# A two-layer graph network on one core: the adjacency's transpose goes from TensorE to VectorE, by way of a second load and DRAM

## The chip, the cores and the metric

The kernel runs on one core of a Trainium2 chip. The metric is the device time of one execution in microseconds (us): before the change a median of 2358.65 us over 3 runs, 2358.03 to 2359.63. A profile is one execution recorded by the hardware profiler. A core has five engines that work through their own instruction lists in order and wait for each other by semaphores: TensorE (PE in the profile, PEld its weight loads), VectorE (DVE), ScalarE (ACT), GpSimd (POOL) and SyncE (SP), which here only issues transfers. TensorE writes its results to PSUM banks, the other data lie in SBUF (128 partitions), and 16 DMA engines move data between SBUF and DRAM.

## The reference

Two layers over B = 16 graphs of N = 1024 nodes with C = 256 channels, all float32. Both share one adjacency `adj` (1024 x 1024).

```python
# layer 0
h = relu(layernorm(x))                       # (16, 1024, 256)
c = mean(h, channel)                         # one number per node
A = (1 - |2 sigmoid(c_j - c_i) - 1|)         # by pairs of nodes, symmetric
g = relu((h^T @ (adj * A)) * para)           # queries
k, v = split(h @ kv_w)                       # keys, values
x = x + softmax(g_head @ k_head^T * scale) @ v_head     # 4 heads
# layer 1
h = relu(layernorm(x))
An = adj + I
deg = colsum(An) + rowsum(An) - diag(An)
agg = (An * deg^-1/2[:, None] * deg^-1/2[None, :]) @ h
x = x + batchnorm(relu(batchnorm(agg @ W1^T + b1)) @ W2^T + b2)
```

Layer 0 uses the rows of `adj` as they lie. Layer 1 needs the transposed, scaled adjacency as the moving operand of TensorE (the tile `ahatT`), and W1 and W2 transposed.

## The kernel before

The batches are taken one after the other. For each there is a graph stage (weights times the rows of h: `f_gps`), keys and values (`f_kps`, `f_vps`), attention in four steps (a half of the queries times a pair of heads: scores `f_s`, exponentials `f_p`, values `f_o`), and a first linear layer of layer 1 for the batch (`linear1`). The second half of the network follows when all batches are through. The order of the instructions on every engine is the order in which the program emits them: the stages run under a manual schedule, and what an engine is to do between the parts of a stage is handed in as lists of steps.

In batch 0 the head runs thus:

- SP loads x of batch 0 in four parts, the eight row blocks of `adj` (`adj_t`, 128 rows each, which stay in SBUF for all batches), kv_w, x of batch 1 and W1 by rows (`load_rows`).
- `graph(0, between)` goes over eight blocks c of nodes. Block c needs a weight tile `w_0_c`: ScalarE makes two activations (L353, L356), VectorE multiplies by the rows of adj (L370), and TensorE makes four products of 128 x 512 (L492). The list `between[c]` holds the steps emitted ahead of block c: weights of later blocks, `turn_h(0)` (h transposed for keys and values, 32 transfers half on SP and half on POOL), and the turns of the adjacency.
- A turn of adjacency block i (`turn_adj` L1372, or `turn_adj_aside` L1383 in other banks) is eight TensorE transposes of 128 x 128 into PSUM. `place_adj` (L1380) or `place_adj_aside` (L1394) copies the result into `ahatT`, in an order of nodes in which node 8u + i lies at place 128 i + u. Seven of the eight copies are VectorE's, one is ScalarE's.
- W1 is turned by VectorE in blocks of 32 x 32 (`turn_weights`, L1452), stored to DRAM by POOL in an order that completes the transpose (L1458), and loaded back by SP into `w1T` (L1491).
- Row sums of the adjacency (L1402, ScalarE, eight) run in `between[4]`.
- After the eight blocks, `graph` runs keys and values of batch 0 (L516 to L552): 14 products in two groups V and K, with ScalarE copies and VectorE additions that free the few PSUM banks.
- `prepare_row(1)` (L307) sends the sums of h of batch 1 to DRAM and loads them back as a row over all partitions, both on SP (L315, L316). The weights of batch 1 use this row in attention step 0 of batch 0.
- Then SP loads x of batch 0 again (`again(0)`, emitted in `between[6]`) and W2 by rows (`w2n`). POOL runs `diagonal()` (L1411: sixteen small operations that pick the diagonal out of `ahatT` and add the identity), VectorE sums it, and POOL loads six small columns (`later`).

In attention of batch 0 the lists `hooks[i]` add work at the end of the scores of step i: weights of batch 1 in steps 0 and 1, two column sums of `ahatT` on ScalarE in every step (L1407), in step 1 the turn of W2 by VectorE (L1452), stored by POOL, in step 2 the sums of W1's blocks (`make_w1_sums`), in step 3 `roots`, which makes deg^-1/2. The row of roots and the scaling of `ahatT` lie in the graph stage of batch 1. VectorE's list for one step is: six additions of exponentials, the hooks, the last addition (L899), a transpose and a reduction of the sums (L907, L915), and the transpose of the step's result out of PSUM (L936), which frees the bank that the values of the next step write.

Pools of tiles hand out buffers in turn: `w4` has five (weights, para, W1, W2), `p` eight (exponentials and others), `oT` two, `att` one, and PSUM has `s` with three double banks, `t` and `o` with one bank each.

Of the kernel before, what the change touches and what calls it, by code (L numbers as in the profile page):

```python
# [10 lines left out]
F32 = mybir.dt.float32  # L11
# [6 lines left out]
P = 128  # L18
# [11 lines left out]
def fast_path(  # L30
# [38 lines left out]
    w1T_d = dram.tile([P, CC, F1], F32, tag="fw1T", name="fw1T")  # L69
    w2T_d = dram.tile([P, FC, C], F32, tag="fw2T", name="fw2T")  # L70
    w1s_d = dram.tile([P, 4, FC * P // 2], F32, tag="fw1s", name="fw1s")
# [108 lines left out]
    with ExitStack() as stage:  # L180
# [19 lines left out]

        adj_t = []
# [105 lines left out]
        def prepare_row(b, behind=lambda: None):  # L307
# [6 lines left out]
            if b > 0:  # L314
                nc.sync.dma_start(row_d[b].rearrange("(c p) -> p c", p=P), sums_of[b])  # L315
                nc.sync.dma_start(row, row_d[b].unsqueeze(0).to_broadcast([P, N]))  # L316
                return
# [155 lines left out]
        def graph(b, between):  # L473
# [42 lines left out]
            if b == 0:  # L516
# [8 lines left out]
                K.copy(0, 0)  # L525
                V.product(6)
# [9 lines left out]
                K.copy(1, 0)  # L536
                V.product(4)
# [13 lines left out]
                K.copy(0, 1)  # L551
                return qT, kT, v  # L552
# [819 lines left out]
        def turn_adj(i):  # L1372
            ps = ps_s.tile([P, NC, P], F32, tag="s", name=f"f_adjps_{i}")
            for m in range(NC):
                nc.tensor.transpose(ps[:, m, :], adj_t[i][:, ts(m, P)], ident)
            turned_adj[i] = ps

        turned_adj = {}

        def place_adj(i, copy):  # L1380
            copy(columns(i), turned_adj.pop(i).rearrange("p m (q i) -> p m i q", i=NC))

        def turn_adj_aside(i):  # L1383

            turned_adj[i] = [
                ps_o.tile([P, NC // 2, P], F32, tag="o", name=f"f_adjpsa_{i}"),
                ps_t.tile([P, NC // 2, P], F32, tag="t", name=f"f_adjpsb_{i}"),
            ]
            for m in range(NC):
                nc.tensor.transpose(  # L1390
                    turned_adj[i][m // 4][:, m % 4, :], adj_t[i][:, ts(m, P)], ident
                )

        def place_adj_aside(i, copy):  # L1394
            for n, ps in enumerate(turned_adj.pop(i)):
                copy(columns(i)[:, 4 * n : 4 * n + 4], ps.rearrange("p m (q i) -> p m i q", i=NC))
# [14 lines left out]
        def diagonal():  # L1411
# [5 lines left out]
            nc.vector.tensor_reduce(diag, on, AX.X, ALU.add)  # L1417
# [44 lines left out]
        with tc.manual_schedule(engines={ENG.PE, ENG.Activation, ENG.DVE, ENG.Pool, ENG.SP}):  # L1462
# [16 lines left out]
            turn_adj(0)  # L1479
            xs[1] = load_x(1)  # L1480
            prepare_row(0, lambda: place_adj(0, nc.vector.tensor_copy))
            turn_adj(1)
            turn_adj_aside(2)
            place_adj(1, nc.vector.tensor_copy)
            weights(0, 1)

            w1n = load_rows(W1, FC, "w1")
            w1T = big.tile([P, CC, F1], F32, tag="w1T", name="f_w1T")

            def load_w1T():  # L1490
                nc.sync.dma_start(w1T, w1T_d)  # L1491
# [5 lines left out]
                    1: [  # L1497
                        lambda: place_adj_aside(2, nc.vector.tensor_copy),
                        lambda: weights(0, 3),
                        lambda: turn_adj(3),  # L1500
                        lambda: place_adj(3, nc.scalar.copy),
                    ],
                    2: [
                        lambda: weights(0, 4),
                        lambda: turn_weights(w1n, unused("w1Q"), w1T_d, FC),
                        lambda: prepare_start(1),
                        lambda: turn_adj_aside(4),
                        lambda: place_adj_aside(4, nc.vector.tensor_copy),
                    ],
                    3: [  # L1510
                        lambda: weights(0, 5),
                        lambda: turn_adj(5),
                        lambda: place_adj(5, nc.vector.tensor_copy),
                    ],
# [1026 lines left out]
```

## Time and profile before

| what | us |
|---|---|
| median of 3 runs | 2358.65 |
| the profiled execution: its own time | 2359.59 |
| its span | 2357.7 |
| TensorE's first transpose of the adjacency | 8.26 |
| first product of the graph stage of batch 0 | 14.41 |
| first product of keys and values | 46.91 |
| first scores of attention, batch 0 | 59.26 |
| first product of the graph stage of batch 1 | 115.60 |
| first product of linear1, batch 0 | 157.82 |

The page gives the busy time of each engine as a share of the span, then the chain of work that ended last, followed back from the last instruction. The answers in order of time have one line for a run of like instructions: start, busy time, engine, line of the kernel, operation, output and inputs, shapes, count, and in brackets the idle time before it and what ended that. The answers by stretch have one line for a stretch of time: its ends, its length, the busy time of PE, PEld, DVE, ACT and POOL with the number of instructions in brackets, the granted clock of TensorE, the share of the 16 DMA engines that was busy, and the GB/s that they moved.

### The profile page before, as it was taken

What the parts mean: (1) busy time and instruction counts of PE and PEld (TensorE: products, weight loads), DVE (VectorE), ACT (ScalarE), POOL (GpSimd) and SP (SyncE); (2) the same over time, 40 slices, a digit from 0 to 9 for tenths busy, and PEclk for the clock granted to TensorE, in tenths of its full rate; (3) what the DMA queues carried; (4) which work ended last, traced back from release to release, by engine and by line L of the source; (5) the groups of instructions that cost most, each with busy time, mean ns of one, the idle gap of its engine ahead of it and who ended that gap; (6) DMA issues with size and microseconds to landing.
All of it is one profiled execution on the core that took longest, in us unless ns stands there. A gap on an engine that the chain in (4) does not pass through costs nothing.

```text
span 2357.7 us, 25774 instructions
## 1 busy us (share of the span) xinstructions
PE 2319.9 (98%) x8256; PEld 1030.6 (44%) x8256; DVE 1994.6 (85%) x2937; ACT 1416.0 (60%) x2057; POOL 447.7 (19%) x573
## 2 busy tenths in 40 slices
PE   8999999999999999999999999999999999999995
PEld 5353444434353534444443434343444434444444
DVE  7988989798979899897989798988989898747766
ACT  7846566574738474655657384746556575346644
POOL 5121222121221122221212221221212121100000
PEclk9999999999999999999999999999999999999998
DMA  7143433434342435335343324253343521455579
GB/s 205 46 143 99 150 127 124 153 110 124 136 132 73 168 90 174 103 134 143 116 143 126 116 97 154 83 177 99 134 143 116 161 72 55 135 209 174 171 242 382
DMA packets 169218, 326.42 MB, mean 138 GB/s; under 512 B 34929, under 2 KB 102001, under 8 KB 169073
## 3 DMA queue, kind: packets, MB, share of 16 engines
q1 hardware_dynamic: 145264, 268.02, 33.3%
q0 software_dynamic: 19200, 39.88, 6.4%
q10 hardware_dynamic: 4608, 16.78, 1.7%
q8 instruction: 67, 1.10, 0.2%
q14 instruction: 79, 0.64, 0.1%
HBM read 203.96 MB, written 101.77 MB: 130 GB/s over the span
## 4 chain that ended last, share of the span: by engine, by line
PE 96%; DMA 1%; DVE 1%; ACT 0%; issue 0%; SPq 0%; ACTq 0%; POOLq 0%; DVEq 0%; POOL 0%
PE f_s L871 19%; PE f_o L923 19%; PE f_aps L1088 16%; PE f_gps L689 8%; PE f_zps L1198 7%; PE f_gpsx L689 6%; PE f_zx L1760 4%; PE f_zm L1760 3%; PE f_vpsx L436 2%; PE f_kpsx L431 2%; PE f_gps L492 2%; PE f_vps L436 2%; PE f_kps L431 2%; PE f_zps L1281 1%; PE f_zps3a L1198 1%; PE f_zps3b L1198 1%
## 5 line engine op out<-in xcount | busy, mean ns | idle before, releaser
L879 ACT ACTIVATE f_p<-f_s 128x1024 f32<-128x1024 f32 x512 | 476.9, 1047 | 59.8 <-PE f_s L871 59.8
L871 PE MATMUL f_s<-f_qT,f_kT 64*128 64x512 f32 x2048 | 456.8, 596 | 0.0
L923 PE MATMUL f_o<-f_p,f_v 128*64 128x512 f32 x2048 | 453.6, 595 | 0.0
L871 PEld LDWEIGHTS f_s<-f_qT,f_kT 64*128 64x128 f32 x2048 | 191.2, 185 | 263.7 <-issue 118.1
L923 PEld LDWEIGHTS f_o<-f_p,f_v 128*64 128x64 f32 x2048 | 141.4, 137 | 304.3 <-issue 265.4
L366 POOL TENSOR_TENSOR f_w<-f_w,f_adj 128x1024 f32<-128x1024 f32 x56 | 132.3, 2363 | 700.8 <-ACT f_w L365 506.6
L991 POOL DMA_DIRECT2D f_att<-f_oT x256 | 136.1, 539 | 342.9 <-DVE f_oT L974 337.3
L894 DVE TENSOR_TENSOR f_acc<-f_acc,f_p 128x1024 f32<-128x1024 f32 x128 | 155.8, 1217 | 4.6 <-ACT f_p L879 4.6
L894 DVE TENSOR_TENSOR f_sums<-f_sums,f_p 128x1024 f32<-128x1024 f32 x128 | 155.7, 1217 | 0.0
L353 ACT ACTIVATE f_w<-f_row,f_col 128x1024 f32<-128x1024 f32 x127 | 147.3, 1160 | 12.0 <-DMA f_row<-frow 7.4
L356 ACT ACTIVATE f_w<-f_w 128x1024 f32<-128x1024 f32 x127 | 134.4, 1058 | 4.0
L1088 PE MATMUL f_aps<-f_ahatT,f_hs 128*128 128x512 f32 x256 | 115.2, 593 | 0.0
L1088 PE MATMUL f_aps<-f_ahatT,f_h_b 128*128 128x512 f32 x256 | 112.6, 592 | 0.0
L1088 PE MATMUL f_aps<-f_t,f_hs 128*128 128x512 f32 x256 | 112.5, 592 | 0.0
L365 ACT ACTIVATE f_w<-f_w,f_now 128x1024 f32<-128x1024 f32 x56 | 64.3, 1148 | 77.5 <-DVE f_now L363 77.5
L689 PE MATMUL f_gps<-f_w,f_h_a 128*128 128x512 f32 x224 | 109.8, 592 | 0.0
L885 DVE TENSOR_TENSOR f_acc<-f_p,f_p 128x1024 f32<-128x1024 f32 x64 | 77.9, 1217 | 24.9 <-ACT f_p L879 24.9
L891 DVE TENSOR_TENSOR f_sums<-f_p,f_p 128x1024 f32<-128x1024 f32 x64 | 78.1, 1221 | 20.2 <-ACT f_p L879 20.1
L370 DVE SCALAR_TENSOR_TENSOR f_w<-f_w,f_adj 128x1024 f32<-128x1024 f32 x71 | 88.0, 1258 | 7.8 <-ACT f_w L356 7.7
L285 ACT ACTIVATE f_h_a<-f_x,f_shift_a,f_rstd_a 128x256 f32<-128x256 f32 x126 | 73.8, 587 | 31.4 <-DVE f_shift_a L270 31.4
L1221 ACT ACTIVATE f_z<-f_zps,f_b 128x512 f32<-128x512 f32 x60 | 37.9, 683 | 75.3 <-PE f_zps L1198 75.3
L285 ACT ACTIVATE f_h_b<-f_x,f_shift_b,f_rstd_b 128x256 f32<-128x256 f32 x128 | 66.2, 592 | 25.8 <-DVE f_shift_b L270 25.8
(297 smaller groups left out, 3983.9 us busy)
## 6 DMA issues: line engine op xcount, KB each, us to landing
f_t<-ft SPq DMA_DIRECT2D x84, 512.0 KB, 9.6
fz<-f_z SPq DMA_DIRECT2D x64, 512.0 KB, 9.8
f_x<-in_x_dram SPq DMA_DIRECT2D x31, 1024.0 KB, 6.3
f_zb<-fz SPq DMA_DIRECT2D x42, 512.0 KB, 4.4
fx<-f_x SPq DMA_DIRECT2D x16, 1024.0 KB, 4.4
fgs<-f_gs POOLq DMA_DIRECT2D x28, 512.0 KB, 3.0
fhT<-f_hQ POOLq DMA_DIRECT2D x112, 128.0 KB, 3.2
f_hT<-fhT SPq DMA_DIRECT2D x28, 512.0 KB, 6.3
```

The costliest lines, as they stand in the source:

```text
L285: nc.scalar.activation(self.h[:, c, :], self.xt[:, c, :], AF.Relu, bias=self.shift[:, c : c + 1], scale=self.rstd[:, c : c + 1], accum_out ...
L353: nc.scalar.activation(w, rows[b], AF.Abs, bias=cols[b][:, c : c + 1], scale=0.5 / C)
L356: nc.scalar.activation(w, w, AF.Tanh)
L689: nc.tensor.matmul(ps, left, right, start=fresh and n == 0, stop=(n == PAIRS - 1), skip_group_check=more,)
L871: nc.tensor.matmul(ps[:, e, :], kT[rows_e, pair, ts(m, P)], qT[rows_e, pair, ts(g, 512)], start=True, stop=True,)
L879: nc.scalar.activation(p, ps, AF.Exp)
L894: nc.vector.tensor_add(to, to, p)
L923: nc.tensor.matmul(o_of[s][e * HD : (e + 1) * HD, :], v[:, m, ts(2 * pair + e, HD)], p[:, e, :], start=(m == 0), stop=(m == NC - 1),)
L991: queue.dma_start(t[ts(j, 32), :, a].rearrange("r h c i -> r h (c i)"), oT[ts(a, 32), :, j].rearrange("r h c i -> r h (c i)"),)
L1088: nc.tensor.matmul(ps, left[:, m, :], right(m), start=not more and m == 0, stop=(m == KH - 1), skip_group_check=more,)
L1198: nc.tensor.matmul(ps[i], left[:, ts(i, P)], right, start=not more, stop=True, skip_group_check=more,)
L1760: nc.tensor.matmul(ps, left[:, m, :], right[:, m, :], start=start and m == 0, stop=(m == 1), skip_group_check=not start,)
```

## The change

The adjacency is no longer turned by TensorE. While the graph stage of batch 0 ends and keys and values are made, SP loads the whole adjacency a second time: eight tiles, each by four transfers of 32 rows, that take every eighth row. VectorE turns each tile in blocks of 32 x 32 into `ahatT`, which serves as a staging place: two turns ahead of the products of keys and values, two in "first", one in "then", three in "end". After turns 3 and 7, POOL stores half of it to a DRAM tensor `adjT_d` in pieces of 512 bytes, four transfers a half. SP loads `adjT_d` back into `ahatT` in four transfers, and behind these x of batch 0 and W2. W1 is loaded behind the first x, turned by TensorE at the place of the first adjacency block, and copied by VectorE straight to `w1T`. The row of batch 1 goes over POOL's queue. The row sums are spread (three in block 4, one in keys and values, two each in steps 0 and 1), the column sums lie in steps 2 and 3 (four each), the six small columns come ahead of the diagonal on POOL, and the diagonal's reduction goes to step 3.

```diff
+        w1T = big.tile([P, CC, F1], F32, tag="w1T", name="f_w1T")
+        w1n = w4.tile([P, FC, C], F32, tag="w4", name="f_w1n")
+        nc.sync.dma_start(w1n, W1.rearrange("(f p) d -> p f d", p=P))
...
             if b > 0:
-                nc.sync.dma_start(row_d[b].rearrange("(c p) -> p c", p=P), sums_of[b])
-                nc.sync.dma_start(row, row_d[b].unsqueeze(0).to_broadcast([P, N]))
+                queue = nc.gpsimd if b == 1 else nc.sync
+                queue.dma_start(row_d[b].rearrange("(c p) -> p c", p=P), sums_of[b])
+                queue.dma_start(row, row_d[b].unsqueeze(0).to_broadcast([P, N]))
...
                 K.copy(0, 0)
+                for step in between["first"]:
+                    step()
...
                 K.copy(1, 0)
+                for step in between["then"]:
+                    step()
...
                 K.copy(0, 1)
+                for step in between["end"]:
+                    step()
...
-        def turn_adj(i):
...
-        def place_adj(i, copy):
...
-        def turn_adj_aside(i):
...
-        def place_adj_aside(i, copy):
...
+        stage_rows = ahatT.rearrange("p m x -> p (m x)").rearrange("p (k t r) -> p k t r", k=32, t=NC)
+        by_rows = adj.rearrange("(u i) d -> i u d", i=NC)
+        def load_adj(t, home):
+            pool, tag, bufs = home
+            to = pool.tile([P, N], F32, tag=tag, name=f"f_adjr_{t}", bufs=bufs)
+            for a in range(4):
+                nc.sync.dma_start(to[ts(a, 32)], by_rows[2 * a + t // 4, ts(t % 4, 32)])
+            adj_rows[t] = to
+        def load_adj_ahead():
+            for t, home in enumerate(((ow, "oT", 2), (ow, "oT", 2), (ow, "att", 1))):
+                load_adj(t, home)
+        def load_adj_behind():
+            for t in range(3, NC):
+                load_adj(t, (w4, "w4", 5))
+        def turn_adj(t):
+            nc.vector.transpose(
+                stage_rows[:, :, t], adj_rows.pop(t).rearrange("p (k s) -> p k s", s=32)
+            )
+        def store_adj(half):
+            to = adjT_d.rearrange("(k s) (a g x) -> g a s k x", s=32, a=4, g=2)[half]
+            for a in range(4):
+                nc.gpsimd.dma_start(
+                    to[a],
+                    stage_rows[ts(a, 32), :, 4 * half : 4 * half + 4].rearrange(
+                        "p k t r -> p k (t r)"
+                    ),
+                )
+        def reload_adj():
+            whole = adjT_d.rearrange("(m p) x -> p m x", p=P)
+            for m in range(0, NC, 2):
+                nc.sync.dma_start(ahatT[:, m : m + 2], whole[:, m : m + 2])
...
-            turn_adj(0)
+            w1ps = ps_s.tile([P, CC, FC, P], F32, tag="s", name="f_w1ps")
+            for d in range(CC):
+                for f in range(FC):
+                    nc.tensor.transpose(w1ps[:, d, f, :], w1n[:, f, ts(d, P)], ident)
...
-                    6: [
-                        lambda: prepare_end(1),
-                        make_key_sums,
-                        load_w1T,
-                        lambda: again(0),
-                    ],
-                    8: [lambda: prepare_row(1)],
+                    4: [lambda: weights(0, 7), *(lambda m=m: row_sums(m) for m in range(3))],
+                    6: [load_adj_ahead, lambda: prepare_end(1), make_key_sums],
+                    8: [
+                        load_adj_behind,
+                        lambda: turn_adj(0),
+                        lambda: turn_adj(1),
+                        lambda: prepare_row(1),
+                    ],
+                    "first": [lambda: turn_adj(2), lambda: turn_adj(3), lambda: store_adj(0)],
+                    "then": [lambda: turn_adj(4), lambda: row_sums(3)],
+                    "end": [
+                        *(lambda t=t: turn_adj(t) for t in range(5, NC)),
+                        lambda: store_adj(1),
+                    ],
                 },
             )
+            reload_adj()
+            again(0)
             w2n = load_rows(W2, CC, "w2")
             w2Q, w1s_t = (w4.tile([P, N], F32, tag="w4", name=f"f_{n}") for n in ("w2Q", "w1s"))
-            diagonal()
             for load in later:
                 load()
+            sum_diagonal = diagonal()
...
-                            hooks.setdefault(m // 2, []).append(lambda m=m: column_sums(m))
+                            hooks.setdefault(2 + m // 4, []).append(lambda m=m: column_sums(m))
+                        for m in range(4, NC):
+                            hooks[1 - m // 6].append(lambda m=m: row_sums(m))
+                        hooks[3].append(sum_diagonal)
                         hooks[1].append(lambda: turn_weights(w2n, w2Q, w2T_d, CC))
```

## The prediction

> **What bounds the kernel now.** I read the page's busy row and the end of the chain first, then the first 165 us of each engine in order of time, then the DMA rates in short stretches.
>
> ```profile
> PE 2319.9 (98%) x8256; PEld 1030.6 (44%) x8256; DVE 1994.6 (85%) x2937; ACT 1416.0 (60%) x2057; POOL 447.7 (19%) x573
> PE 96%; DMA 1%; DVE 1%; ACT 0%; issue 0%; SPq 0%; ACTq 0%; POOLq 0%; DVEq 0%; POOL 0%
> ```
>
> TensorE is the chain: only what removes TensorE work, or makes it wait, counts. In order of time, TensorE's head:
>
> ```profile
> 8.26 1.94 PE L1375 MATMUL f_adjps<-f_ident,f_adj 128*128 128x128 f32 x8 [8.26 <-DMA f_adj<-in_adj_dram]
> 12.24 1.04 PE L1375 MATMUL f_adjps<-f_ident,f_adj 128*128 128x128 f32 x8
> ...
> 14.41 3.67 PE L492 MATMUL f_gps<-f_w,f_h_a 128*128 128x512 f32 x8 [0.26 <-DVE f_w L339]
> 17.91 1.04 PE L1375 MATMUL f_adjps<-f_ident,f_adj 128*128 128x128 f32 x8
> 18.79 3.60 PE L492 MATMUL f_gps<-f_w,f_h_a 128*128 128x512 f32 x8
> ...
> 59.26 7.14 PE L871 MATMUL f_s<-f_qT,f_kT 64*128 64x512 f32 x32
> ...
> 94.50 7.09 PE L923 MATMUL f_o<-f_p,f_v 128*64 128x512 f32 x32
> ```
>
> The first three blocks of the adjacency (8.26, 12.24, 13.11) are turned while TensorE waits for the first weights anyway (0.26 on L339 remains). Blocks 3 to 7 stand between products.
>
> **What it removes.** Starts of those five are 0.88, 1.10, 0.87, 0.87 and 0.87 us ahead of the next product (17.91 to 18.79, 22.58 to 23.68, and so on): 4.6 us off TensorE. The eight W1 transposes take the place of block 0 at 8.26, before TensorE waits for the sums at 9.99: nothing. The gap at 12.24 becomes idle, since the first weights (L339, 13.58) hang on ScalarE and the row copy, not on TensorE: nothing won there. The cover holds if the weights keep up with one product per 3.5 us: ScalarE makes a block in 2.13 us (starts 14.06, 16.19, 18.32) and VectorE masks it in 1.2, with six PSUM copies of 1.2 us and W1's turn (1.24) fewer to do. W1's way through DRAM goes too (SP 5.1 us, POOL 2.5 us of issue), all of it beside TensorE: nothing. So attention starts at 59.26 - 4.6 = 54.7. That is the whole gain, 0.19% of 2358.65; 0.2% (4.7 us) is about what a measurement of this kernel can tell from no change.
>
> **The second load.** SP issues 32 transfers of 128 KB behind the two of para (31.8, 32.3). Nearest row for the issue: f_w2n, 0.42 each; for the rate, the stretch in which only w2n (32 partitions a transfer, as here) is moving:
>
> ```profile
> 12.00:14.00 2.00, 2.00 (x20) 1.91 (x18) 1.59 (x3) 1.94 (x4) 0.00 (x0) 1.00 1.04 424
> 63.00:64.00 1.00, 1.00 (x6) 0.38 (x4) 0.69 (x1) 1.00 (x2) 0.00 (x0) 1.00 1.00 242
> ```
>
> The last number is GB/s, the one before it the DMA share: the engines are full at 242 with 32 partitions, and at 424 with the 128 partitions of the first adjacency load. The Trainium skill, SBUF — State Buffer, section "Door 1: The DMA port swizzle", says that 32 partitions reach only half of the ports and gives 189 GB/s at 1 MiB, 218 at best. A tile of 0.52 MB takes 2.2 us by the row and 2.8 by the rule; I take the row, and keep the rule for the range, as it speaks against this change.
>
> From 33.1 (first bytes of para): para 2.8, then tiles at 38.2, 40.4, 42.6, the key sums' store 1.4, tiles 3 to 7 at 46 to 55, each landing 0.7 later. VectorE's deadlines: turns 0 and 1 stand ahead of the two para products (L521), which free the bank of K's first product (TensorE 44.2 after the change), so tile 1 must land by 41.7 (it does at 41.1; 0 to 0.7 us at risk). Turns 2 and 3 stand ahead of K.add(0,0,2) and the V.adds that free the bank for K.product(4) at 52.9: tile 3 by 49.7. Turn 4: by 53.3. A turn is 1.2 us (f_w2Q below, 1.24). VectorE has over 5 us of waits between 47 and 58, so these turns fit: nothing. The last three follow K's last add (54.8) and end at T7 = 58.6, delaying the first attention sums by about 1 us, which its waits of 1.73 and 0.61 there absorb.
>
> **The way back, where the cost is.** store_adj(1) goes out at T7. Each half is 2.1 MB in pieces of 512 bytes, 32 partitions a transfer: at 230 GB/s (between 200, fw2T's 256-byte pieces at full share, 131 to 184 GB/s at shares 0.7 to 0.9, and 242) 9.1 us, after 2 us of POOL's issue (fw2T: 0.74 with half the pieces, first bytes 0.5 later). SP's reload waits for all eight stores, R = 58.6 + 2 + 9.1 + 0.7 = 70.4. But the first half is stored from about 48 to 60 while tiles 4 to 7 are still loading. Sharing costs: the 1 MB load of x lands after 5.5 us at 44.0, and after 10.2 at 197.1 beside three stores of 512 KB, with 400 GB/s of both together. Loads, row and first store add up to 33 us of full DMA, 33.1 to 66.5; fully shared, tile 7 comes at 64 and R = 76.5. I take R = 74.
>
> Behind the reload in SP's order stand x of batch 0 and w2n. Bytes after R: 4.2 MB at 405 GB/s (stretches of the first load) 10.4 us, x 1.05 MB at 331 (46 to 48 us) 3.2, w2n 2.2, first bytes 1.3, landing 0.7, and 1 for the six columns of small pieces (0.5 of the DMA share after 50 us before): 18.8. So w2n lands at L = 93 (89 to 96 by the two ends of R). Before, it was there by 67. VectorE wants it at 85.24 - 4.6 = 80.7:
>
> ```profile
> 85.24 1.24 DVE L1452 STREAM_TRANSPOSE f_w2Q<-f_w2n 128x1024 f32<-128x1024 f32 x1
> 90.04 0.71 DVE L936 STREAM_TRANSPOSE f_oT<-f_o 128x512 f32<-128x512 f32 x1
> ...
> 100.94 1.02 ACT L965 COPY f_recs<-f_rec 32x32 f32<-32x32 f32 x4 [1.67 <-DVE f_rec L957]
> 102.75 7.44 ACT L879 ACTIVATE f_p<-f_s 128x1024 f32<-128x1024 f32 x8 [0.78 <-PE f_s L871]
> ```
>
> Behind the w2 turn on VectorE are: the last sum of step 1, its two reductions, and the transpose that frees the f_o bank, 5.5 us in all (85.24 to 90.7); values of step 2 (94.50 before, 89.9 now) wait for it. Then the sums of step 2 and the reciprocals, for which ScalarE waits (L965) before the exponentials of step 3. Slack of that chain: VectorE's waits of 0.56 and 0.28 in step 2 plus the 0.78 above, 1.6 us; so w2n is free of cost until 82.3, and from there VectorE has no wait left up to 126 us, so each us late is a us on TensorE. Cost at 93: 10.7.
>
> **The rest.** The diagonal (POOL, 16 operations of 0.5 to 1.0) starts when the first reload lands, about 78, and ends by 90, before ScalarE's column sums (92.5 or later): nothing; later than that, it stalls ScalarE one for one. Four column sums in step 2, for two: +2.1 against waits of 1.67 and 0.78: nothing. Row sums take the place of column sums in steps 0 and 1, two for two: nothing. In step 3 VectorE gains the diagonal's reduce (1.2) in a stretch without waits, and the mask of block 2 ended 1.2 ahead of its product (121.4, 122.6): 0 to 0.6, I take 0.6. The row leaves SP (which waited 13.6 us there) for POOL, about 37; landing in 5 to 14 us and loading in 6.5, it is there by 58, needed at 63; POOL's stores stand behind it, at worst 4 us later.
>
> A wait of some 8 us on TensorE has its own price. The skill, TensorE: Matmul & The Clock Gate, section "What's actually happening", says that an idle window of about 3.4 us halves the clock until a busy one has passed. The row: the eight transposes at 8.26 after idling take 1.94, later eights 1.04, while the granted clock reads 1.00. By the rule +1.7, by the clock row 0; I take 1.2, since VectorE's queue hides part.
>
> Sum on the profiled execution: 2359.6 - 4.6 + 10.7 + 0.6 + 1.2 = 2367.5; it ran 0.9 over the median of 2358.65 (span 2357.7 plus 1.9 outside), so 2366.5 as a median.
>
> **Rivals.**
> 1. w2n does not queue behind the reload in the DMA engines but shares them from its own issue, some 3 us after R: it then lands about 8 us after that, 81.5 with R at 70.4, in time by the 82.3 above, and the removal stands: 2358.65 - 4.6 + 0.6, about 2354.5, not slower. For it: w2n and the row, issued together at 59, landed together at 65. Against: in the first load each of the later transfers on this queue took 10 to 11 us to land behind 4 MB of adjacency (x of batch 1 11.1, kv_w 10.4). Chance 0.06.
> 2. Loads and stores overlap without slowing each other (different directions): R about 68 to 70, L 84 to 89, time 2357 to 2362, centre 2359.5: gain and wait cancel. For it: two queues moving 32-partition pieces at once (f_hT, f_att) stay at 0.44 to 0.54 of the DMA share, 122 to 130 us. Chance 0.23.
> 3. The waits grow: 512-byte writes or 32 partitions at the rule's 189 GB/s put R at 82 and L near 101, and tile 1 and tile 7 then stall keys, values and step 1 too: 2358.65 - 4.6 + 18.7 + 2.5, about 2375. Chance 0.15.
> The forecast has 0.56, with its own range of 2362 to 2371. That the change would remove no TensorE time I rule out: the products follow each other.
>
> **How the numbers follow.** Range: rival 1 lies outside below and most of rival 3 above: 2357.0 to 2374.5. Faster by over 0.2% (below 2353.9) needs more than the whole gain: 0.03. Within 0.2%: the rest of rival 1 (0.03), rival 2 (0.23), and the forecast's lower tail (0.07): 0.33. Slower (above 2363.4): 0.64.
>
> **What would show it.** Right: scores start near 54.7; VectorE's largest new wait is at the w2 turn, "<- DMA f_w2n", some 12 us, and TensorE waits at values of step 2 for VectorE's transpose; the reload issues at about 74. Wrong: w2n landed before 82, or the largest wait sits at an adjacency turn between keys and values, or on ScalarE's column sums behind POOL.

## The result and the profile after

The changed kernel takes a median of 2382.12 us (6 runs, 2379.9 to 2383.22) beside 2358.79 for the kernel before (6 runs, 2358.03 to 2359.63): a ratio of 1.0097, 95% interval 1.0084 to 1.011. It is 23.3 us slower. The prediction said slower, 2366.5, with a range up to 2374.5: the sign is right, the size is not.

The profile after is an execution of 2379.9 us (span 2378.1). Its busy row and the end of its chain:

```profile
PE 2321.4 (98%) x8200; PEld 1028.4 (43%) x8200; DVE 1992.5 (84%) x2935; ACT 1415.8 (60%) x2056; POOL 451.7 (19%) x579
PE 92%; DMA 3%; DVE 2%; SPq 1%; issue 1%; ACT 1%; POOL 0%; ACTq 0%; DVEq 0%; POOLq 0%
```

TensorE has 56 matmuls fewer and yet 1.5 us more busy time. The chain, followed back, is off TensorE for 8% of the span where it was 4%, about 95 us more: from the weights of graph(1) it runs back through VectorE's late work in the attention to the load of w2n, the reload, the second store and the tiles of the second load. TensorE in order of time, start and duration first, the wait before it in brackets:

```profile
8.98 1.94 PE L1508 MATMUL f_w1ps<-f_ident,f_w1n 128*128 128x128 f32 x8 [8.98 <-DMA f_w1n<-in_L_gnn_W_dram]
10.71 1.91 PE L325 MATMUL f_rps<-f_ident,f_sums 128*128 128x128 f32 x8
12.41 1.65 PE L331 MATMUL f_rps<-f_ident,f_sums 128*128 128x128 f32 x8
16.07 29.40 PE L497 MATMUL f_gps<-f_w,f_h_a 128*128 128x512 f32 x64 [2.00 <-DVE f_w L344]
...
53.57 2.07 PE L436 MATMUL f_kpsx<-f_hT,f_kvw 128*128 128x512 f32 x2 [6.32 <-DVE f_qT L526]
55.43 1.91 PE L441 MATMUL f_vpsx<-f_kvs,f_kt 128*128 128x128 f32 x8
...
67.21 7.14 PE L882 MATMUL f_s<-f_qT,f_kT 64*128 64x512 f32 x32 [0.68 <-ACT f_kT L451]
...
114.10 9.73 PE L934 MATMUL f_o<-f_p,f_v 128*64 128x512 f32 x32 [11.58 <-DVE f_oT L947]
```

Starts of the stages on TensorE say where the time went:

| first work of | before | after | shift | added by the stage ahead of it |
|---|---|---|---|---|
| graph(0), first product | 14.41 | 16.07 | +1.66 | +1.66 |
| keys and values of batch 0 | 46.91 | 45.30 | -1.61 | -3.27 |
| attention of batch 0 | 59.26 | 67.21 | +7.95 | +9.56 |
| graph(1) | 115.60 | 137.84 | +22.24 | +14.29 |
| linear1, batch 0 | 157.82 | 180.59 | +22.77 | +0.53 |

The shift then stays between 22.7 and 22.9 us up to 2102.86, the start of the last products with W1, and agrees with the 23.3 of the medians. (The two profiled spans differ by 20.4 only, because TensorE waits less for ScalarE in the last stage of that one execution.) So two stages make the loss: keys and values, and the attention of batch 0. VectorE's new waits show what each waited for:

```profile
41.66 1.25 DVE L1404 STREAM_TRANSPOSE f_ahatT<-f_adjr 128x1024 f32<-128x1024 f32 x1 [3.25 <-DMA f_adjr<-in_adj_dram]
51.09 1.25 DVE L1404 STREAM_TRANSPOSE f_ahatT<-f_adjr 128x1024 f32<-128x1024 f32 x1 [8.19 <-DMA f_adjr<-in_adj_dram]
...
73.42 1.25 DVE L1404 STREAM_TRANSPOSE f_ahatT<-f_adjr 128x1024 f32<-128x1024 f32 x1 [4.40 <-DMA f_adjr<-in_adj_dram]
...
108.54 1.25 DVE L1478 STREAM_TRANSPOSE f_w2Q<-f_w2n 128x1024 f32<-128x1024 f32 x1 [13.74 <-DMA f_w2n<-in_L_gnn_W_dram]
```

The first two are tiles 0 and 1, the third is tile 7, the last is the wait that the prediction named. The queues behind it, POOL's and then SP's (the first line of SP's is from before, the others are after):

```profile
38.74 0.96 POOL L320 DMA_DIRECT2D frow<-f_sums  x1 [5.32 <-ACT f_h_a L289]
50.98 0.58 POOL L321 DMA_DIRECT2D f_row<-frow  x1 [11.27 <-DMA frow<-f_sums]
...
74.97 3.12 POOL L1412 DMA_DIRECT2D fadjT<-f_ahatT  x4 [12.29 <-DVE f_ahatT L1404]
```

```profile
31.79 4.49 SPq L485 DMA_DIRECT2D f_para<-in_L_gnn_para_dram  x2
...
32.39 3.16 SPq L490 DMA_DIRECT2D f_para<-in_L_gnn_para_dram  x2
35.59 6.27 SPq L1392 DMA_DIRECT2D f_adjr<-in_adj_dram  x12
...
89.45 2.12 SPq L1422 DMA_DIRECT2D f_ahatT<-fadjT  x4
91.68 0.45 SPq L195 DMA_DIRECT2D f_x<-in_x_dram  x1
92.17 7.86 SPq L1471 DMA_DIRECT2D f_w2n<-in_L_gnn_W_dram  x4
```

Between the two issues of para SP waits for a graph product (f_gps), 3.5 us before and 2.2 after, and the second load stands behind them. The second store goes out at 74.97 and the reload at 89.45, 14.5 us later. In short stretches (granted clock, DMA share and GB/s are the last three numbers):

```profile
44.00:46.00 2.00, 2.00 (x11) 1.26 (x10) 0.00 (x0) 0.00 (x0) 0.00 (x0) 1.00 0.89 37
46.00:48.00 2.00, 1.25 (x12) 1.06 (x10) 0.00 (x0) 0.59 (x1) 0.00 (x0) 1.00 0.78 35
48.00:50.00 2.00, 0.00 (x0) 0.00 (x0) 0.00 (x0) 0.00 (x0) 0.00 (x0) 1.00 0.72 72
50.00:52.00 2.00, 0.00 (x0) 0.00 (x0) 0.91 (x1) 0.00 (x0) 0.58 (x1) 0.80 0.80 250
52.00:54.00 2.00, 0.43 (x1) 0.43 (x2) 2.00 (x4) 0.00 (x0) 0.00 (x0) 0.50 1.04 301
...
110.00:112.00 2.00, 0.00 (x0) 0.00 (x0) 1.97 (x2) 0.00 (x0) 1.92 (x3) 0.50 0.40 59
```

Two things stand here. From 44 to 50 the engines are 0.7 to 0.9 busy and move 35 to 72 GB/s, while tile 1 is outstanding, and so is frow: 4 KB in 1024 pieces of 4 bytes, issued at 38.74 and landed 11.9 us later. The profile books that busy time on SP's queue and almost none on POOL's, so the trace alone does not say what slows SP's transfers. And after each long wait of TensorE the granted clock reads 0.50.

### The profile page after: what moved, and what is told of

Read it like the earlier page. It is cut to its first block, busy times and chain, and to the rows that moved or that the text cites. A ratio compares the mean times of both kernels' runs of the same rounds, so it can differ in the third digit from the quotient of the medians.

```text
span 2378.1 us, 25724 instructions
## 1 busy us (share of the span) xinstructions
PE 2321.4 (98%) x8200; PEld 1028.4 (43%) x8200; DVE 1992.5 (84%) x2935; ACT 1415.8 (60%) x2056; POOL 451.7 (19%) x579
## 4 chain that ended last, share of the span: by engine, by line
PE 92%; DMA 3%; DVE 2%; SPq 1%; issue 1%; ACT 1%; POOL 0%; ACTq 0%; DVEq 0%; POOLq 0%
PE f_s L882 18%; PE f_o L934 18%; PE f_aps L1099 16%; PE f_gps L700 8%; PE f_zps L1209 6%; PE f_gpsx L700 6%; PE f_zx L1776 4%; PE f_zm L1776 3%; PE f_vpsx L441 2%; PE f_kpsx L436 2%; PE f_gps L497 2%; PE f_vps L441 2%; PE f_kps L436 2%; DMA f_adjr<-in_adj_dram 1%; PE f_zps L1292 1%
## 5 line engine op out<-in xcount | busy, mean ns | idle before, releaser
L934 PE MATMUL f_o<-f_p,f_v 128*64 128x512 f32 x2048 | 456.2, 598 | 11.6 <-DVE f_oT L947 11.6
L371 POOL TENSOR_TENSOR f_w<-f_w,f_adj 128x1024 f32<-128x1024 f32 x56 | 132.4, 2364 | 701.2 <-ACT f_w L370 528.3
```

The costliest lines, as they stand in the source:

```text
L934: nc.tensor.matmul(o_of[s][e * HD : (e + 1) * HD, :], v[:, m, ts(2 * pair + e, HD)], p[:, e, :], start=(m == 0), stop=(m == NC - 1),)
```

## The experiments

Each kernel ran beside the kernel before on the same chip; times are medians, with the ratio to before. The medians of the kernel before in the five groups of runs lie between 2358.44 and 2358.93, so kernels of different groups can be compared to about half a microsecond and their own scatter.

### The two waits, apart and together

```diff
# w2n_ahead
+            w2n = load_rows(W2, CC, "w2")
             reload_adj()
             again(0)
-            w2n = load_rows(W2, CC, "w2")
# row_wide (batch 1 alone)
-                queue.dma_start(row_d[b].rearrange("(c p) -> p c", p=P), sums_of[b])
+                view = "(p c) -> p c" if b == 1 else "(c p) -> p c"
+                queue.dma_start(row_d[b].rearrange(view, p=P), sums_of[b])
```

> The changed kernel with one edit: SP issues the four transfers of w2n ahead of the reload instead of behind it and x; nothing is left out. Theory (the wait for w2n costs the 11.6 us that TensorE waits at values of step 2, and 2.6 us more because the clock is at half behind it): w2n is there before VectorE wants it at 94.8, both go, 2382 - 14 = 2368 us (2366 to 2370). Rival (what stands behind the reload is late anyway, so the wait moves to ScalarE's column sums or to the scale of the adjacency): 2374 us or more, with a new wait in attention of batch 0. A third, that the two transfers stand in each other's way so that the reload is later by as much as w2n took, gives 2368 as well, but with the reload issued 3 us later.

> The changed kernel with the sums of batch 1 written to frow as 128 pieces of 32 bytes instead of 1024 of 4 bytes; the order of the numbers in the row of batch 1 is then another one, so this part is not computed as it should be, with the same instructions otherwise. Theory (the pieces of 4 bytes occupy the DMA engines while tile 1 of the second load is in their queues): frow lands within 4 us, tile 1 at about 43 instead of 51.1, keys and values take 14 to 16 us instead of 21.9, and the total falls by 6 to 8 us, to about 2375, the wait for w2n staying at 11 to 14 us since the reload moves up along with the rest. Rival (loads of 32 partitions, para and the key sums' store crowd each other, whatever frow does): tile 1 stays within 1.5 us of 51, 2381 to 2383.

> Both edits: w2n ahead of the reload, and frow in 128 pieces of 32 bytes (the row of batch 1 is not in the right order; the rest is computed). Theory (two waits that add up, each with its own cause): 2382 - 14 - 7 = 2361 us (2358 to 2364). Rival (they are one wait: what is won in keys and values is lost again at tiles 5 to 7, the reload or the column sums): 2366 to 2370, as with w2n ahead alone.

| kernel | us | ratio (95%) | against the changed kernel |
|---|---|---|---|
| w2n_ahead | 2371.55 | 1.0053 (1.0036 to 1.007) | -10.6 |
| row_wide | 2375.68 | 1.0069 (1.0052 to 1.0086) | -6.4 |
| both | 2365.64 | 1.0028 (1.0019 to 1.0038) | -16.5 |

They add up (-17.0 by sum), so they are two waits with two causes, as the theory of both has it; its time, 2365.64, is above the 2358 to 2364 that the theory gave. VectorE and two stretches of row_wide:

```profile
45.55 1.25 DVE L1405 STREAM_TRANSPOSE f_ahatT<-f_adjr 128x1024 f32<-128x1024 f32 x1 [0.95 <-DMA f_adjr<-in_adj_dram]
...
42.00:44.00 2.00, 2.00 (x6) 0.85 (x5) 0.66 (x1) 0.00 (x0) 0.00 (x0) 1.00 1.06 232
44.00:46.00 2.00, 2.00 (x6) 0.86 (x5) 1.04 (x2) 0.00 (x0) 0.53 (x1) 1.00 1.06 232
```

With the same bytes in pieces of 32 bytes, tile 1 is there at 45.55 instead of 51.09 (9.2 us after the start of the second load instead of 15.5), and the stretch from 44 to 46 moves 232 GB/s instead of 37. TensorE's wait in front of K's first product is gone, and keys and values take 13.8 us (46.05 to 59.87) instead of 21.9. That 4 KB of small pieces on POOL's queue held back the megabytes on SP's is shown, though not by what means; the rival, that loads of 32 partitions crowd themselves, is out. With w2n ahead, TensorE's 11.58 us in front of the values of step 2 are gone, but the gain is 10.6, not 14: a new wait of 2.48 for ScalarE stands in step 3, and in both one of 3.21. (The reload is issued at 90.42, 1.0 us later, and not the 3 of the third theory.) ScalarE itself waits there for VectorE, so neither the theory nor the rival named has it right.

### The diagonal

In both, VectorE, POOL, ScalarE and TensorE in step 2 and at the start of step 3:

```profile
98.90 1.54 DVE L906 TENSOR_TENSOR f_acc<-f_acc,f_p 128x1024 f32<-128x1024 f32 x1
...
97.86 1.50 POOL L1442 TENSOR_TENSOR f_unused_d<-f_ahatT,f_ident 128x128 f32<-128x128 f32 x1
...
107.74 1.02 ACT L977 COPY f_recs<-f_rec 32x32 f32<-32x32 f32 x4 [4.10 <-DVE f_rec L969]
...
109.86 5.94 PE L883 MATMUL f_s<-f_qT,f_kT 64*128 64x512 f32 x20 [3.21 <-ACT f_p L891]
```

VectorE's sums take 1.54 us while POOL works on the diagonal, and POOL's operations 1.4 to 1.5; elsewhere they take 1.22 and 0.52.

```diff
# no_diag, on top of both
-            for m in range(NC):
-                block = columns(m)[:, m]
-                nc.gpsimd.tensor_mul(as_columns(on[:, m, :]), block, as_columns(ident))
-                nc.gpsimd.tensor_add(block, block, as_columns(ident))
+            nc.scalar.activation(on.rearrange("p m q -> p (m q)"), adj_t[0], AF.Copy)
```

> On top of both (w2n ahead, frow in 32-byte pieces: 2365.6): the sixteen operations of the diagonal on POOL are left out, one copy on ScalarE fills their scratch tile instead, so the diagonal, its sum and the identity are not computed. Theory (POOL and VectorE slow each other: while the diagonal runs, VectorE's sums over 128x1024 take 1.54 us instead of 1.22 and the POOL operations 1.4 to 1.5 instead of 0.5, which makes VectorE about 2.8 us late with the reciprocals of step 2, for which ScalarE waits 4.10 and TensorE 3.21): sums back at 1.22, TensorE's wait in step 3 below 0.5, total 2361.5 (2360.5 to 2363). Rival (the four column sums on ScalarE in step 2, two more than before, are what is late): the wait stays, 2365 to 2366.5.

2361.43 us, ratio 1.0011 (1.0004 to 1.0018), 4.2 below both. The head and the same places:

```profile
16.87 27.70 PE L498 MATMUL f_gps<-f_w,f_h_a 128*128 128x512 f32 x64 [2.01 <-DVE f_w L345]
...
98.21 1.22 DVE L906 TENSOR_TENSOR f_sums<-f_sums,f_p 128x1024 f32<-128x1024 f32 x1
...
106.21 4.79 PE L883 MATMUL f_s<-f_qT,f_kT 64*128 64x512 f32 x20 [0.62 <-ACT f_p L891]
```

The four column sums are still there, most of the wait is not: the theory holds, though the 0.62 that is left is more than its 0.5. Not all of the 4.2 is the diagonal's: from the scores of step 2 to graph(1) the two profiled executions differ by 3.75 us (33.04 and 29.29). Most of the rest lies in steps 0 and 1, where the diagonal has not begun: in this execution the graph products were not slowed (27.70, 29.40 in both), and SP began the second load at 34.70 instead of 35.75. The changed kernel does not show this cost, because there POOL works on the diagonal from 94.66 to 104.8, inside VectorE's wait for w2n (94.8 to 108.5). One loss covered another.

### The second store

```diff
# cols_behind
-            for load in later:
-                load()
             sum_diagonal = diagonal()
+            for load in later:
+                load()
# store_wide (both halves to contiguous places; the first half's transfer is left out here)
-            to = adjT_d.rearrange("(k s) (a g x) -> g a s k x", s=32, a=4, g=2)[half]
+            to = adjT_d.rearrange("(g a s k) n -> g a s k n", g=2, a=4, s=32)[half]
...
+                if half == 1:
+                    nc.gpsimd.dma_start(to[a], ahatT[ts(a, 32), 4:8])
+                    continue
```

> The changed kernel with one edit: POOL issues the six loads of columns (pieces of 4 bytes) behind the diagonal instead of ahead of it, so that they no longer run beside the second store; nothing is left out. Theory (pieces of 4 bytes slow the store as they slowed tile 1): the reload is issued 3 to 4 us earlier than 89.45, and since w2n hangs on it one for one, the total falls to 2378.5 (2377.5 to 2380). Rival (512-byte pieces of 32 partitions are slow by themselves): the reload moves by less than 1 us, 2381 to 2383.

> The changed kernel with the second store written from contiguous 16 KB of each partition instead of 32 pieces of 512 bytes, same 2.1 MB, same 32 partitions a transfer, same issue; both halves go to contiguous places in memory, so the adjacency of batch 0 comes back in a wrong order and is not the transposed one. Theory (the pieces of 512 bytes hold the store at 150 to 205 GB/s with full engines, where 32 partitions alone allow 242 to 250): from issue to landing 10 to 11 us instead of 14, reload at about 86, total 2379 (2378 to 2380). Rival (32 partitions, or the way to memory, hold it): reload within 1 us of 89.45, 2381 to 2383.

cols_behind: 2381.68 us, ratio 1.0098 (1.0081 to 1.0115). The theory falls. Its second store is issued at 76.90 and its reload at 91.02, 14.1 us later (14.5 in the changed kernel), with nothing else in the engines:

```profile
81.00:83.00 2.00, 2.00 (x12) 0.62 (x10) 2.00 (x3) 2.00 (x4) 0.00 (x0) 1.00 0.95 154
83.00:85.00 2.00, 2.00 (x10) 0.83 (x10) 2.00 (x3) 1.12 (x3) 0.00 (x0) 1.00 0.94 172
85.00:87.00 2.00, 2.00 (x12) 0.93 (x10) 1.93 (x3) 2.00 (x3) 0.00 (x0) 1.00 1.01 205
87.00:89.00 2.00, 2.00 (x12) 0.92 (x12) 2.00 (x3) 2.00 (x3) 0.00 (x0) 1.00 1.01 176
```

So the store alone fills the engines at 154 to 205 GB/s, about 175: 2.1 MB take 12 us. store_wide: 2377.45 us, ratio 1.0079 (1.0062 to 1.0095), 4.7 below the changed kernel and below even the 2378 to 2380 of its theory:

```profile
82.00:84.00 2.00, 2.00 (x12) 0.65 (x10) 2.00 (x2) 1.81 (x4) 0.67 (x1) 1.00 1.01 389
84.00:86.00 2.00, 2.00 (x12) 0.91 (x10) 2.00 (x3) 1.41 (x2) 0.71 (x1) 1.00 1.05 436
```

With 16 KB pieces the same full engines move 389 to 436 GB/s, and TensorE's wait in front of the values of step 2 falls from 11.58 to 5.51. This is not the store alone: with its contiguous layout half of the reload no longer depends on the second half of the store and runs beside it. The profile splits the traffic by queue, though. From 82 to 86 us the store's queue moved 1.16 MB in 69.8% of the engines' time; in cols_behind it moved 2.10 MB in 82.5% of the 14 us from 77 to 91. As an estimate from these, that is some 415 and 182 GB/s with full engines, both with 32 partitions a transfer. So, by this estimate, it is the pieces of 512 bytes that limit the store, by their size or by where they lie in DRAM, and not the 32 partitions.

### The head

```diff
# unturned (the kernel before; likewise blocks 4 to 7)
-                        lambda: turn_adj(3),
-                        lambda: place_adj(3, nc.scalar.copy),
+                        lambda: place_unturned(3, nc.scalar.copy),   # copies adj_t[3] as it is
# early, on top of both
-                    0: [lambda: weights(0, 2), lambda: turn_h(0)],
+                    0: [load_adj_ahead, lambda: weights(0, 2), lambda: turn_h(0)],
...
-                    6: [load_adj_ahead, lambda: prepare_end(1), make_key_sums],
+                    6: [lambda: prepare_end(1), make_key_sums],
# early_warm, on top of early: ahead of f_w_0_0
+            for name, pool in (("o", ps_o), ("t", ps_t)):
+                aside = pool.tile([P, 4, P], F32, tag=name, name=f"f_aside_{name}")
+                for c in range(8):
+                    nc.tensor.transpose(aside[:, c % 4, :], w1n[:, c % 4, ts(c // 4, P)], ident)
```

> The kernel before, with the forty transposes of blocks 3 to 7 of the adjacency left out: the blocks are copied into their places as they are, so the transposed adjacency of batch 0 and all that follows from it is not computed as it should be; copies, loads and everything else stay. Theory of the forecast (five blocks of 0.87 to 1.10 us stand between products and nothing else is behind them): scores start at 54.7, total 2358.7 - 4.6 = 2354.1 (2353.5 to 2355). Rival (the gain is partly lost to a later wait, or the blocks stood where TensorE would have waited anyway): 2355.5 to 2358.7.

> On top of both (2365.6): SP issues the twelve transfers of tiles 0 to 2 of the second load ahead of those of h, at about 12 us, where its queue and the DMA engines have little to do; nothing more is left out. Theory (the second load is late because it starts at 35.7 and everything behind it, tile 7 and the stores too, moves with it): VectorE's waits for tiles 0 and 1 (4.16 and 0.95) go, tile 7 lands about 5 us earlier than 69.2, so TensorE's waits in step 0 (0.54 and 1.25, with slower matmuls behind them) go, 2362 (2361 to 2363.5). Rival (the early tiles only push x of batch 1 and the transfers of h back, or the end of the load is set by the first store that shares the engines with it): tile 7 at 67 or later, 2364.5 or more.

> On top of early: sixteen more transposes of blocks of w1n, whose results nobody reads, fill the idle 2 us of TensorE ahead of the first product. Theory (the first products run at half clock because TensorE idled before them; that is where 1.7 us of the 4.6 went): the 64 products take 27.6 us instead of 29.4 and the total is 1.5 to 2 us below that of early. Rival (the weights, made by ScalarE in 2.13 us a block and masked by VectorE, set the pace of the first products, so that a faster clock only waits more): the 64 products take as long, total within 0.5 us of early.

unturned: 2357.57 us, ratio 0.9996 (0.9988 to 1.0005). Of the 4.6 us off TensorE nothing measurable is left, as the rival has it. Keys and values start at 43.79, 3.1 earlier than before, but then TensorE waits, and the operations of VectorE that it waits for are slow ones:

```profile
42.97 1.00 DVE L458 TENSOR_TENSOR f_kt<-f_hT,f_hT 128x512 f32<-128x512 f32 x1
...
48.32 1.12 PE L431 MATMUL f_kpsx<-f_hT,f_kvw 128*128 128x512 f32 x2 [2.58 <-DVE f_qT L521]
```

The sum at 42.97 takes 1.00 us, while POOL works on the diagonal beside it; in the changed kernel, where the diagonal comes later, the same sum takes 0.69. So in the kernel before, by these traces, VectorE was level with TensorE at this place, and less work on TensorE alone could not buy the time.

early: 2362.89 us, ratio 1.0017 (1.001 to 1.0024), 2.8 below both, as its theory has it. Scores start at 57.21, ahead of the 59.26 of before, tile 7 comes at 66.0, and TensorE's waits in steps 0 and 1 (0.54 and 1.25) shrink to one of 0.49; the wait of step 3 (3.07) stays, as it should with the diagonal still there. early_warm: 2362.32 us, ratio 1.0015 (1.0008 to 1.0022), 0.6 below early and not the 1.5 to 2 of the theory; but the reason is not the rival's:

```profile
16.43 27.70 PE L502 MATMUL f_gps<-f_w,f_h_a 128*128 128x512 f32 x64 [0.26 <-DVE f_w L349]
...
49.62 1.13 PE L441 MATMUL f_kpsx<-f_hT,f_kvw 128*128 128x512 f32 x2 [3.69 <-DVE f_qT L531]
...
41.52 0.29 DVE L1185 TENSOR_TENSOR f_kvs<-f_kvw 128x128 f32<-128x128 f32 x1 [6.04 <-DMA f_hT<-f_hQ]
```

The 64 products take 27.70 instead of 29.40, as the theory has it. In this profiled execution the gain is lost again because VectorE waits for h, whose transfers stand behind the twelve early ones (SP issues them from 29.0 on, in early from 26.6; 21.9 to 23.0 where SP loads no tiles ahead of them). Part of that lateness is this execution's own: its first load landed 1.3 us later than early's (10.07 and 8.80).

### Can the loss be removed?

all_fixes and all_fixes_store put the edits above together, take the products for the diagonal from the first load (before keys and values), let POOL issue tiles 0 to 2 at about 10 us, and keep frow in its proper order by a strided read on ScalarE.

> Everything is computed. The changed kernel with: w2n ahead of the reload; frow in 32-byte pieces, with ScalarE reading the row of batch 1 in the matching order; tiles 0 to 2 of the second load issued by POOL ahead of the transfers of h; the eight products for the diagonal taken from the first load of the adjacency, on POOL ahead of keys and values, and their sum on VectorE ahead of the last turn; the idle of TensorE ahead of the first product filled with sixteen transposes. Theory (the waits found are the whole of the loss, and the 4.6 us off TensorE then stand, less some slowing of VectorE by the eight additions left on POOL): 2355.5 (2354 to 2357.5), scores start at 54 to 55. Rival (the work moved early slows what stands there, as the early tiles pushed h back, or the additions on POOL still make VectorE late in step 2): 2359 to 2362, with TensorE waiting for f_qT in keys and values or for ScalarE in step 3.

> As all_fixes, with the first store issued behind turn 4 instead of behind turn 3, so that it shares the engines with less of the second load; everything is computed. Theory (the first store keeps tile 7 back, and with it the sums of step 0): tile 7 two to four us earlier, total 0.5 to 1 us below all_fixes. Rival (the stores end later by as much, and the reload, the diagonal and the column sums with them): the same or up to 2 us above.

2369.87 us (ratio 1.0046, 1.0029 to 1.0063) and 2369.51 (1.0044, 1.0027 to 1.0061): the theory falls, both are above the rival's 2359 to 2362 as well, and the later store changes nothing measurable. By the trace, two of the edits cost more than they were to give:

```profile
34.16 2.71 DVE L261 BATCH_NORM_STATS2 f_st_a<-f_x 128x6 f32<-128x256 f32 x8 [6.23 <-DMA f_x<-in_x_dram]
...
71.40 2.24 ACT L367 ACTIVATE f_w<-f_row,f_col 128x1024 f32<-128x1024 f32 x1
```

The early tiles held up x of batch 1 (to 34) and h, and reading the row with a stride of 32 bytes took ScalarE 2.24 us where a plain read takes 1.14. VectorE then waits up to 1.93 for each weight tile of batch 1, and TensorE 3.48 for VectorE in the keys of batch 1. combined drops both: tiles 0 to 2 go between h and para, and VectorE turns the sums, so that frow is written in 128-byte pieces in its own order:

```diff
# combined, the row of batch 1
+                    wide, turned = row[:, :32], row[:, 32:64]
+                    nc.vector.memset(wide, 0.0)
+                    nc.vector.tensor_copy(wide[:, :NC], sums_of[b])
+                    nc.vector.transpose(turned, wide)
+                    to = row_d[b].rearrange("(c a i) -> a c i", c=NC, a=4)
+                    for a in range(4):
+                        queue.dma_start(to[a], turned[32 * a : 32 * a + NC])
```

> Everything is computed. The changed kernel with: w2n ahead of the reload; the sums of batch 1 turned by VectorE in blocks of 32x32, so that frow is written in 32 pieces of 128 bytes in its proper order; tiles 0 to 2 of the second load issued by SP behind the transfers of h and ahead of para; the products of the diagonal taken from the first load ahead of keys and values and summed ahead of the last turn; both stores behind the last turn; sixteen transposes in the idle ahead of the first product. Theory (early tiles and a strided row, not the other edits, cost all_fixes its gain): x of batch 1 and h arrive as before, scores start at 55 to 56, no wait over 1 us in the attention of batch 0, 2356 (2354.5 to 2358). Rival (the second load and the way back through memory need more time of the DMA engines than the first 100 us have to spare, wherever they are put): 2359 to 2363, with a wait for a transfer in graph, keys or values, or with ScalarE's column sums late.

2359.09 us, ratio 1.0002 (0.9993 to 1.001): level with the kernel before, 23 us better than the changed one, and at the edge of the rival's range. Behind its first scores, the attention of batch 0 has no wait over 0.3 us. Its head:

```profile
15.20 27.70 PE L510 MATMUL f_gps<-f_w,f_h_a 128*128 128x512 f32 x64 [0.26 <-DVE f_w L357]
...
45.74 1.22 DVE L539 TENSOR_TENSOR f_qT<-f_gps,f_para 128x1024 f32<-128x1024 f32 x1 [3.27 <-DMA f_para<-in_L_gnn_para_dram]
...
58.96 1.99 PE L895 MATMUL f_s<-f_qT,f_kT 64*128 64x512 f32 x8 [0.67 <-ACT f_kT L464]
```

Keys and values start at 42.74, 4.2 earlier than before, and scores at 58.96, 0.3 earlier: now para is late, because the tiles went ahead of it. Each place that was tried for the second load made another transfer of the head late. No version here is measurably faster than the kernel before.

## Why the prediction was wrong

Direction and main mechanism hold: w2n queued behind the reload, VectorE's w2 turn waiting for it, TensorE waiting at the values of step 2. The terms of the sum, which measured come to 22.7 us, the shift of the table above:

| term | forecast, us | measured, us |
|---|---|---|
| off TensorE in graph(0), with the head | -4.6 | -1.6 |
| keys and values | 0 | +9.6 |
| wait for w2n on TensorE | +10.7 | +11.6 |
| clock behind that wait | +1.2 | +2.6 |
| graph(1), mask | +0.6 | +0.5 |

- **"The gap at 12.24 becomes idle ...: nothing won there" was read as nothing lost.** The transposes of blocks 1 and 2 had kept TensorE busy up to its first product. Without them it idles 2.0 us, and the products begin at half clock (granted 0.50 from 18 to 20 us); early_warm prices that at 1.7 us (29.40 against 27.70). It does not come every time: in no_diag the same idle of 2.01 us was followed by products at full speed, and why stays open. The first product starts 1.66 later, because w1n landed at 8.98 (the block of before at 8.26) and the transposes ahead of it ran slowly too (1.91 and 1.65 for 1.53 and 1.04).
- **Tile 1 "by 41.7 (it does at 41.1; 0 to 0.7 us at risk)" was the costliest step.** Its turn began at 51.09. Two terms failed. First, the load started 3 us late: SP issued para's second half at 35.2 and not at 32.3, since it waits for a graph product and the head was late and slow. TensorE was as late, so this alone cost little: in row_wide tile 1 came at 45.55 and TensorE did not wait for it. Second, frow was costed as a transfer of its own ("landing in 5 to 14 us", right with 11.9), not as one that keeps the engines from others. Beside its small pieces the tile took 6.3 us longer (15.5 against 9.2 from the start of the load), and TensorE waited 6.32; the half clock behind that cost another 2.3. The deadline itself, the bank of K's first product, was right. The wait reached TensorE through VectorE's order: the turn of tile 1 stands ahead of the products with para, which do not read it. No run put it behind them.
- **The rate of the tiles was right, on a doubtful row.** 232 GB/s at full share in row_wide, from 42 to 44 us too, where almost nothing but tiles was moving, stands by the 242 of the row taken. In that stretch of before, f_row of batch 1 was still on its way as well, so it did not show w2n alone. The 189 to 218 that the Trainium skill's page SBUF — State Buffer, section "Door 1: The DMA port swizzle", gives for 32 partitions are not seen in these loads, of which several, on different partitions, were in the engines at once.
- **"Each half is 2.1 MB ... at 230 GB/s ... 9.1 us" was too fast.** cols_behind gives about 175 GB/s and 12 us. From T7 to R the sum without sharing has 11.8 us, and 14.8 were measured; that the 3.6 us added to R for the tiles loading beside the first store just cover this is luck. With T7 at 74.7 instead of 58.6, R is 89.45. As the wait counts from where VectorE wants w2n, and that moved as well (80.7 to 94.8), only the difference costs.
- **"Behind R ... 18.8" was right:** 19.1 (89.45 to 108.54). (The later end of its L comes to 95.3 and not 96.) The slack was nearly so (1.6 forecast): a wait of 13.74 on VectorE cost TensorE 11.58.
- **The clock: "by the clock row 0; I take 1.2" took the wrong side.** Values of step 2 took 9.73 for 7.09, the first products of K and V 5.5 for 3.1, and the head lost 1.7: 6.7 in three places. The granted clock does show it (0.50 from 52 to 58 and from 106 to 118), but not in the first 14 us, where the forecast looked and where transposes take up to twice as long beside a 1.00. The Trainium skill's page TensorE: Matmul & The Clock Gate, section "What's actually happening", gives the rule from which the prediction had +1.7 for such a wait. The runs are on its side, with 1.7, 2.3 and 2.6 in place of one figure, and none in the head of no_diag.
- **"The diagonal: nothing" was right by cover alone.** The prediction asked whether POOL would make ScalarE late and left out that POOL and VectorE slow each other. The Trainium skill's page SBUF — State Buffer, section "Who interferes with whom", says that a VectorE instruction with two inputs from SBUF contends with a GpSimd instruction that reads SBUF. Here it is 1.54 for 1.22 and 1.4 to 1.5 for 0.52, and about 3.7 us of the kernel once w2n is in time. The trace of before had it already: f_kt took 1.00 there beside the diagonal, where the changed kernel, with POOL idle, takes 0.69.
- **Rival 3 (2375, "tile 1 and tile 7 then stall keys, values and step 1 too") was the nearest.** It had the right places and 2.5 us for them, where keys and values alone cost 9.6. Its chance of 0.15 was too low, as a landing 0.6 us ahead of a deadline had no margin.

## What to carry to other kernels

Before moving work to a transfer, list for each transfer what else is in the DMA engines at that moment, by number of pieces and not only by bytes, and treat a landing that is forecast within a microsecond of its deadline as late. A rearrangement that frees TensorE also takes away what kept its clock up and what kept POOL out of VectorE's way, so price the idle that it leaves. Ask, too, whether the work that waits for the transfer has to stand ahead of work that does not need it. Where one loss hides another, as the wait for w2n hid the diagonal here, repairing the first gives less than its length in the trace.

## What the runs showed of the hardware

- 1024 pieces of 4 bytes on POOL's queue took 11.9 us to land. While they were on their way the engines were 0.72 to 0.89 busy at 35 to 72 GB/s, and a tile of 0.52 MB on SP's queue came 15.5 us after the start of its load, against 9.2 beside 128 pieces of 32 bytes.
- A store in pieces of 512 bytes filled the engines at 154 to 205 GB/s, where loads in 4 KB rows, 32 partitions a transfer too, reached 232, and a store in 16 KB pieces some 415 (an estimate from its share of the engines' time).
- An activation on ScalarE that reads 4-byte numbers 32 bytes apart took 2.2 us for 128x1024, against 1.14 for the same numbers side by side.
- TensorE's first transposes took 1.94 and 1.91 us for eight, against 1.04 later, while the granted clock read 1.00; after 16 us the row shows the half-clock stretches. An idle of 2.0 us ahead of the first product was followed by half clock in the changed kernel and by full speed in no_diag.
